# A selective-scan kernel in which TensorE forms part of dt*u*B with diagonal matrices

## The chip, the cores and the metric

The kernel runs on one core of a Trainium2 chip. The metric is the device time of one execution in microseconds (us). A core has five engines that run side by side, each taking its own instructions in order: TensorE (PE, matrix products into PSUM), VectorE (DVE), ScalarE (ACT), GpSimd (POOL) and SyncE (SP, which here only starts transfers). They wait for each other through semaphores.

## What is computed

The reference is one layer of a bidirectional state-space model over 16 sequences of 512 positions with 256 features, followed by a soft mixture of 16 experts. Inside the first half, 512 channels with 16 states each go through a scan along the sequence, once forward and once backward. Cut to what matters:

```python
dA = jnp.einsum('bld,dn->bldn', dt, A)
dB_u = jnp.einsum('bld,bld,bln->bldn', dt, u, B)
...
xs = jnp.cumsum(dB_u * dA_cum, 1) / (dA_cum + 1e-12)
y = jnp.einsum('bldn,bln->bld', xs, C)
```

`dB_u` is, for each state n, the product dt*u of a channel times B of that state, which depends on the position alone. The kernel writes the scan as a recurrence: h = h * exp(dt*A) + dt*u*B at each position, and takes (1 + tanh(...)) * h * C, summed over the states, for the division by `dA_cum + 1e-12`. After it come a gate, an output projection, a layer norm, the experts (dispatch by a softmax over positions, two matrices with a gelu, a third matrix, combination by a softmax over 1024 slots) and a last layer norm.

## The kernel before, in words

A sequence has four *parts*: `scan_part` for forward and backward (r = 0, 1) and for two pairs of channel chunks of 128 (p = 0, 1), in the order (0,0), (1,0), (0,1), (1,1). A part runs over state pairs n = 0, 2, ... 14 and, in each, over its two chunks. One such *step* covers 128 channels x 512 positions x 2 states, and there are 16 x 4 x 16 = 1024 of them. In a step:

- SP loads, once for both chunks, the rows of B and C of two states, spread over 128 partitions: `bs` (three buffers) and `cs` (two buffers), line 352.
- POOL multiplies `db` = du * bs, two states at once, 1024 elements per partition (line 356; three buffers).
- For each of the two states ScalarE makes the decay exp(dt*A) in a PSUM tile `h` (line 361; a ring of three banks) and `th`, a tanh (line 363). VectorE scans in place in h, with db as the term that is added (line 365 forward, 367 backward), and then writes hg = (th + 1) * h (line 370; four buffers of two states).
- POOL multiplies hg by cs in place (line 371).
- TensorE transposes hg by blocks of 128 and adds it up in the PSUM tile `acc` (line 320), two steps after the step that made it (`add_up(2)`). The first step of a chunk also gets u*D by a matmul with a diagonal matrix (line 333).

Everything else is *side work*, written as generators that yield between pieces and are emitted a piece at a time after each step (`beside_scan`): preparation of the next part (`prep_*`: projections, convolution, silu, softplus, and `prep_pair`, which makes dt, rr and, on POOL, du = dt*u), the end of the sequence before with the experts' dispatch (`finish`, `dispatch`), and the experts and the combination (`experts`, `combine`) of pairs of sequences. The side work shares three PSUM banks (`bank`, tag `mps`). A piece says how many banks it takes; `Side.piece` starts it only if, counted from the oldest bank that is still held, no more than three are in use. A piece that ends with HOLD keeps its bank until the generator is taken up again. `late` pins an instruction to program order on its engine; the others may be moved by the framework's scheduler. With the pools `m_acc` (two banks) and `m_h` (three) the eight banks are given out.

`prep_pair` of a part runs during the part before. `project_unit` (line 240) makes `xd`, which holds the rows of B and C, and writes them to DRAM as `bc`, from where `bs` and `cs` are read. `experts` loads its weights into three buffers with the tag `W` (line 644). `combine` gathers the experts' outputs of one sequence from DRAM into one tile `ceo` of 8 x 257 columns (line 814), whose last column is set to one, so that the matmul at line 844 gives the sum of the softmax weights in column 257; VectorE takes its reciprocal (line 853) before it scales (line 854). After the last scan a tail runs with all eight banks: the experts and the combination of the last two sequences.

## Time and profile before

| | |
|---|---|
| runs of the kernel before, us | 5466.05, 5471.18, 5471.56 (median 5471.18) |
| the profiled execution's own time, us | 5474.83 |
| its span, first to last instruction, us | 5473.0 |
| mean granted TensorE clock | 0.859 |
| first db starts, last db starts, us | 47.5, 5166.5 |
| ScalarE waiting for VectorE's hg (line 361 for line 370), us | 609.8 in 488 waits |
| TensorE waiting for POOL's hg (line 320), us | 312.9 in 145 waits |
| SP waiting for POOL before bs and cs (for lines 371 and 356), us | 2542.8 and 940.9 |
| ceo from its issue to its landing, us | 7.0 |

How to read it: the profile lists groups of instructions by line, engine and tile, with total busy time and mean time of one, and the idle time that its engine had just before such an instruction, with what ended it. Busy shares are averages over the span; tables by stretch tell the stages apart. Durations on POOL are rough, matmuls are pipelined, and idle time of an engine that doesn't set the pace costs nothing.

### The profile page before, as it was taken

How to read it: one execution, taken by the hardware profiler on the slowest of the kernel's cores; microseconds unless marked ns; L12 is line 12 of the kernel's file. 1: busy time of each engine (PE TensorE's matmuls, PEld its weight loads, DVE VectorE, ACT ScalarE, POOL GpSimd, SP SyncE). 2: the span in 40 equal slices, each digit the busy share in tenths (PEclk: the TensorE clock that was granted, in tenths of full speed). 3: DMA queues.
4: the chain of work that ended last, by engine and by line, in shares of the span. 5: the costliest groups of instructions: out<-in, count | busy, mean ns of one | idle time of the engine just before them, and what ended most of it. 6: DMA issues, size and time to landing. Idle time of an engine off the chain costs nothing.

```text
span 5473.0 us, 67758 instructions
## 1 busy us (share of the span) xinstructions
PE 4001.2 (73%) x21317; PEld 3106.7 (57%) x21330; DVE 4522.5 (83%) x6212; ACT 4101.0 (75%) x6665; POOL 5003.5 (91%) x2547
## 2 busy tenths in 40 slices
PE   4556656677787777777777777877777776778887
PEld 2434444565555665566556655555655665567656
DVE  6787878889898888888888898989888888888722
ACT  6667777778778777878777887787778787778641
POOL 6999999999999999999999999999999999989700
PEclk7567777888998998889899888988988898999999
DMA  4333333465546664366544655455544666457435
GB/s 131 112 112 123 122 118 121 157 206 186 166 137 193 198 191 150 131 205 208 177 138 157 204 186 170 136 193 193 192 149 136 200 203 189 139 168 250 135 104 174
DMA packets 493949, 897.77 MB, mean 164 GB/s; under 512 B 44403, under 2 KB 291827, under 8 KB 493589
## 3 DMA queue, kind: packets, MB, share of 16 engines
q1 hardware_dynamic: 454836, 851.48, 48.4%
q10 hardware_dynamic: 38752, 41.95, 2.2%
q8 instruction: 169, 2.77, 0.2%
q14 instruction: 192, 1.56, 0.1%
HBM read 832.47 MB, written 60.82 MB: 163 GB/s over the span
## 4 chain that ended last, share of the span: by engine, by line
DVE 33%; ACT 24%; PE 19%; issue 11%; POOL 10%; DMA 3%; SPq 0%; DVEq 0%; ACTq 0%; POOLq 0%
DVE h L367 9%; DVE h L365 8%; DVE hg L370 8%; ACT h L361 5%; ACT th L363 5%; POOL db L356 4%; POOL hg L371 4%; PE acc L320 3%; PE px L247 2%; PE pg L718 2%; DVE rr L302 2%; PE cl L770 2%; ACT L361 2%; PE peo L703 2%; ACT ht L740 1%
## 5 line engine op out<-in xcount | busy, mean ns | idle before, releaser
L356 POOL TENSOR_TENSOR db<-du,bs 128x1024 f32<-128x1024 f32 x1024 | 2424.6, 2368 | 118.9 <-DVE h L365 50.5
L371 POOL TENSOR_TENSOR hg<-hg,cs 128x1024 f32<-128x1024 f32 x1024 | 2422.2, 2365 | 26.2 <-DVE hg L370 17.6
L370 DVE SCALAR_TENSOR_TENSOR hg<-th,h 128x512 f32<-128x512 f32 x2048 | 1349.1, 678 | 253.4 <-ACT th L363 139.7
L320 PE MATMUL acc<-ident,hg 128*128 128x128 f32 x8192 | 1219.4, 302 | 383.9 <-POOL hg L371 312.9
L320 PEld LDWEIGHTS acc<-ident,hg 128*128 128x128 f32 x8192 | 1074.4, 158 | 622.3 <-POOL hg L371 402.3
L367 DVE TENSOR_TENSOR_SCAN h<-h,db 128x512 f32<-128x512 f32 x1024 | 1226.2, 1219 | 191.5 <-ACT h L361 148.3
L365 DVE TENSOR_TENSOR_SCAN h<-h,db 128x512 f32<-128x512 f32 x1024 | 1221.6, 1219 | 181.9 <-ACT h L361 134.1
L361 ACT ACTIVATE h<-dt,A_f 128x512 f32<-128x512 f32 x1024 | 700.0, 684 | 316.6 <-DVE hg L370 313.8
L361 ACT ACTIVATE h<-dt,A_b 128x512 f32<-128x512 f32 x1024 | 699.8, 683 | 297.6 <-DVE hg L370 296.1
L363 ACT ACTIVATE th<-rr,Ah_b 128x512 f32<-128x512 f32 x1024 | 728.0, 711 | 0.3
L363 ACT ACTIVATE th<-rr,Ah_f 128x512 f32<-128x512 f32 x1024 | 726.9, 710 | 0.2
L703 PE MATMUL peo<-Wd,ht 128*128 128x256 f32 x1024 | 321.0, 469 | 196.2 <-DVE ht L687 136.0
L703 PEld LDWEIGHTS peo<-Wd,ht 128*128 128x128 f32 x1024 | 227.4, 232 | 269.7 <-DVE ht L687 143.0
L718 PE MATMUL pg<-st,Wg 128*128 128x128 f32 x2048 | 280.1, 300 | 77.4 <-ACT xb L222 39.7
L770 PE MATMUL cl<-seT,cx 128*128 128x512 f32 x512 | 275.7, 681 | 74.0 <-DVE rr L302 35.7
L718 PEld LDWEIGHTS pg<-st,Wg 128*128 128x128 f32 x2048 | 270.5, 215 | 87.5 <-ACT xb L222 41.2
L675 PE MATMUL pu<-st,Wu 128*128 128x128 f32 x2048 | 268.7, 287 | 30.4 <-ACT ht L740 11.8
L675 PEld LDWEIGHTS pu<-st,Wu 128*128 128x128 f32 x2048 | 256.5, 202 | 52.5 <-ACT ht L740 13.2
L574 PE MATMUL pl<-x2T,seT 128*128 128x512 f32 x512 | 260.0, 632 | 24.3 <-DVE xf L171 14.6
L606 PE MATMUL pq<-dis,xn 128*128 128x256 f32 x1024 | 254.6, 406 | 15.4 <-ACT dis L596 12.7
L844 PE MATMUL cpo<-ceo,ct 128*128 128x257 f32 x1024 | 244.1, 393 | 25.5 <-ACT ct L799 16.4
L606 PEld LDWEIGHTS pq<-dis,xn 128*128 128x128 f32 x1024 | 206.3, 207 | 49.8 <-ACT dis L596 15.6
(147 smaller groups left out, 5149.9 us busy)
## 6 DMA issues: line engine op xcount, KB each, us to landing
bs<-bc SPq DMA_DIRECT2D x512, 512.0 KB, 4.6
cs<-bc SPq DMA_DIRECT2D x512, 512.0 KB, 3.7
Wg<-in_Wg_dram SPq DMA_DIRECT2D x128, 512.0 KB, 5.4
Wu<-in_Wu_dram SPq DMA_DIRECT2D x128, 512.0 KB, 5.8
Wd<-in_Wd_dram SPq DMA_DIRECT2D x128, 512.0 KB, 5.9
bd<-in_bd_dram SPq DMA_DIRECT2D x128, 128.0 KB, 4.7
s_dram<-sl ACTq DMA_DIRECT2D x64, 256.0 KB, 3.0
st<-s_dram SPq DMA_DIRECT2D x128, 128.0 KB, 4.5
```

What stands on the lines that cost most here:

```text
L320: ins = nc.tensor.matmul(accs[c][:, s], hc[:, j, s], ident, is_transpose=True, start=False, stop=(last and j == 1 and lc == NL - 1),)
L356: nc.gpsimd.tensor_tensor(db, du.unsqueeze(1).to_broadcast([P, 2, L]), bs, ALU.mult)
L361: nc.scalar.activation(h, dt, AF.Exp, scale=w["A"][:, c, s])
L363: nc.scalar.activation(th, rr, AF.Tanh, bias=LN_1E12 / 2, scale=w["Ah"][:, c, s])
L365: nc.vector.tensor_tensor_scan(h, h, db[:, j, :], 0.0, ALU.mult, ALU.add)
L367: nc.vector.tensor_tensor_scan(h[:, ::-1], h[:, ::-1], db[:, j, ::-1], 0.0, ALU.mult, ALU.add)
L370: nc.vector.scalar_tensor_tensor(hg[:, j, :], th, 1.0, h, ALU.add, ALU.mult)
L371: nc.gpsimd.tensor_tensor(hg, hg, cs, ALU.mult)
L606: nc.tensor.matmul(pq[:, k * 256 : (k + 1) * 256], xn[:, lc, k * P : (k + 1) * P], dis[:, lc, :], start=(lc == 0), stop=(lc == NL - 1),)
L675: nc.tensor.matmul(pu[:, fc * P : (fc + 1) * P], got["Wu", e][:, k, fc * P : (fc + 1) * P], st[:, k, :, j * SL : (j + 1) * SL], start=(k = ...
L703: nc.tensor.matmul(po[:, :DM], ht[:, fc, :], got["Wd", e][:, fc, :], start=(fc == 0), stop=(fc == NF - 1))
L718: nc.tensor.matmul(pg[:, fc * P : (fc + 1) * P], got["Wg", e][:, k, fc * P : (fc + 1) * P], st[:, k, :, j * SL : (j + 1) * SL], start=(k = ...
```

## The change

In each part two of the sixteen states, 5 and 13 (`DIAG`), no longer get their dt*u*B from POOL. In the state pairs n = 4 and n = 12, `bs` and `db` hold one state (k = 1). The second state's term is made by TensorE: `duT`, the transposed du, times a 128 x 128 matrix with B on its diagonal, for each of four blocks of positions.

- The diagonal matrices stand in DRAM (`diag_dram`). They are cleared once at the start by four transfers from a zero tile on ScalarE's queue. `project_unit` then writes the B rows of the two states onto the diagonals, element by element (1024 elements of 4 bytes), from ScalarE's queue. A pair before its use, SP loads such a set of four blocks as `dg` (128 x 512, one buffer).
- `turn_pair`, a new generator ahead of the other preparation of a part, transposes the part's two du tiles through the banks of the side work; ScalarE copies them to `duT`.
- `by_diagonal` takes a bank of the side work (`hd`) and makes the four matmuls one step ahead of the step that uses them. The planner counts that bank as held (`diags`) until the step is over. In that step ScalarE writes the decay into an SBUF tile `dec` (two buffers) instead of an h tile, and VectorE scans into the bank.
- `combine` takes its experts' outputs in two tiles of four slot groups each, in buffers of the tag `W` (in the tail, in a pool of four). The column of ones is gone: the sum of the weights comes out of the exp itself (`accum_out`), with a small sum and the reciprocal on VectorE in `weights`.
- Tiles of side work (yt, et, sl, the bias rows) share a tag `fr` with two buffers, and the slot embeddings are loaded in two halves into `W` buffers.

```diff
+DIAG = (5, 13)
+DIAG_SIZE = P * (P + 1)
...
+        diag_dram = drams.tile([2, len(DIAG), NL, DIAG_SIZE], F32, name="diag_dram")
...
+        blank = p2.tile([P, 4 * DM], F32, tag="W", name="blank", bufs=3)
+        nc.vector.memset(blank, 0.0)
+        for part in diag_dram.rearrange("r i l (p s) -> (r i) p l s", p=P):
+            nc.scalar.dma_start(part, blank[:, : NL * (P + 1)].rearrange("p (l s) -> p l s", l=NL))
...
+            step = DIAG[1] - DIAG[0]
+            nc.scalar.dma_start(
+                diag_dram[r].rearrange("i l (p s) -> i l p s", p=P)[:, :, :, 0],
+                xd[XB + DIAG[0] : XB + NS : step, :].rearrange("i (l p) -> i l p", p=P),
+            )
...
+        def turn_pair(b, r, p, v):
+
+            yield 2
+            pts = []
+            for c in (2 * p, 2 * p + 1):
+                pt = bank(f"pdu_{b}_{r}_{c}")
+                for lc in range(NL):
+                    s = slice(lc * P, (lc + 1) * P)
+                    nc.tensor.transpose(pt[:, s], v[c][2][:, s], ident)
+                pts.append((c, pt))
+            yield HOLD
+            for c, pt in pts:
+                duT = p4.tile([P, L], F32, tag="duT", name=f"duT_{b}_{r}_{c}", bufs=2)
+                late(nc.scalar.copy(duT, pt))
+                v[c].append(duT)
...
             prep.drain()
-            prep.gens += [[1, g] for g in then]
+            prep.gens += [[1, g] for g in [turn_pair(b, r, p, v)] + then]
...
+            def by_diagonal(n, c):
+
+                diags.append(count[0])
+                made[n, c] = h = bank(f"hd_{b}_{r}_{n}_{c}")
+                for lc in range(NL):
+                    s = slice(lc * P, (lc + 1) * P)
+                    ins = nc.tensor.matmul(h[:, s], v[c][3][:, s], dg[:, s], start=True, stop=True)
+                    if lc == 0:
+                        late(ins)
...
+                k = 1 if n + 1 in DIAG else 2
...
+                if n + 3 in DIAG:
+                    dg = p4.tile([P, L], F32, tag="dg", name=f"dg_{q}", bufs=1)
+                    nc.sync.dma_start(
...
-                    nc.gpsimd.tensor_tensor(db, du.unsqueeze(1).to_broadcast([P, 2, L]), bs, ALU.mult)
+                    nc.gpsimd.tensor_tensor(
+                        db[:, :k, :], du.unsqueeze(1).to_broadcast([P, k, L]), bs[:, :k, :], ALU.mult
+                    )
...
-                        h = ps_h.tile([P, L], F32, tag="h", name=f"h_{q}_{c}_{j}")
-                        nc.scalar.activation(h, dt, AF.Exp, scale=w["A"][:, c, s])
+                        if j < k:
+                            dec = h = ps_h.tile([P, L], F32, tag="h", name=f"h_{q}_{c}_{j}")
+                            add = db[:, j, :]
+                        else:
+                            add = h = made.pop((n + j, c))
+                            dec = p4.tile([P, L], F32, tag="dec", name=f"dec_{q}_{c}", bufs=2)
+                        nc.scalar.activation(dec, dt, AF.Exp, scale=w["A"][:, c, s])
...
+                    nxt_n = n if c == chunks[0] else n + 2
+                    if nxt_n + 1 in DIAG:
+                        for x in sides:
+                            x.take_up()
+                        by_diagonal(nxt_n + 1, chunks[1] if c == chunks[0] else chunks[0])
                     beside_scan()
+                    if k == 1:
+                        diags.pop(0)
...
-                    oldest = min([x.hold for x in sides if x.hold is not None], default=count[0])
+                    oldest = min([x.hold for x in sides if x.hold is not None] + diags[:1], default=count[0])
...
-            for cm, cl in zip(cms, cls):
-                nc.scalar.activation(cm, cl, AF.Exp, bias=nm[:, 2:3])
+            sm = p3.tile([P, 3], F32, tag="csm", name=f"csm_{i}", bufs=2 * NL)
+            for h, (cm, cl) in enumerate(zip(cms, cls)):
+                nc.scalar.activation(cm, cl, AF.Exp, bias=nm[:, 2:3], accum_out=sm[:, h : h + 1])
...
+            for c0 in range(0, NSC, 4):
+                if wide:
+                    t = wide[0].tile([P, 4, DM], F32, tag="ceo", name=f"ceo_{b}_{c0}", bufs=4)
+                else:
+                    t = p2.tile([P, 4 * DM], F32, tag="W", name=f"ceo_{b}_{c0}", bufs=3)
+                    t = t.rearrange("p (c o) -> p c o", c=4)
+                for j in range(2):
+                    nc.sync.dma_start(t[j * SL : (j + 1) * SL, :, :], own[j][:, c0 : c0 + 4, :])
```

## The prediction

> **What bounds the kernel now.** I read the page's list of costliest groups first, then busy time by stretch, then who waited for whom.
>
> ```profile
> PE 4001.2 (73%) x21317; PEld 3106.7 (57%) x21330; DVE 4522.5 (83%) x6212; ACT 4101.0 (75%) x6665; POOL 5003.5 (91%) x2547
> L356 POOL TENSOR_TENSOR db<-du,bs 128x1024 f32<-128x1024 f32 x1024 | 2424.6, 2368 | 118.9 <-DVE h L365 50.5 <-issue 47.8 <-DVE h L367 10.8
> L371 POOL TENSOR_TENSOR hg<-hg,cs 128x1024 f32<-128x1024 f32 x1024 | 2422.2, 2365 | 26.2 <-DVE hg L370 17.6 <-PE cl L770 3.2 <-DVE c_mv L50 2.9
> ```
>
> There are 1024 steps (16 sequences, 64 parts, 16 steps each), and in each POOL spends 2368 + 2365 = 4733 ns on two products. The first db starts at 47.5 us (the db tile's view) and the last hg ends near 5186, so a step takes 5138/1024 = 5.02 us, 94% of it these two; with `du` and small operations POOL is busy about 4982 of 5138 us. Some 156 us are left idle. POOL is the bound, but not in every stretch (columns: stretch, length, busy PE, PEld, DVE, ACT, POOL, clock, DMA share, GB/s):
>
> ```profile
> 3360.00:3440.00 80.00, 66.77 (x317) 46.81 (x318) 75.20 (x106) 62.30 (x103) 80.00 (x38) 0.91 0.38 129
> 3440.00:3520.00 80.00, 57.98 (x279) 40.62 (x279) 69.00 (x93) 64.11 (x103) 77.35 (x42) 0.91 0.47 146
> 3520.00:3600.00 80.00, 59.31 (x313) 43.70 (x312) 69.44 (x99) 65.07 (x109) 73.36 (x38) 0.89 0.40 136
> 3600.00:3680.00 80.00, 59.10 (x385) 51.85 (x384) 67.81 (x95) 63.34 (x101) 79.50 (x46) 0.89 0.60 192
> ```
>
> Two things to see. VectorE can run at 94% (75.20 of 80) with POOL never idle, and its usual share is 85 to 88%. And one stretch in four starves POOL (73.36 of 80): of the 63 such stretches from 80 to 5120 us, 16 have POOL below 94.5%, and in 39 it is at 97% or more. What starves it (timeline: start, length, engine, what), and two lines of the list of waits (total, times, longest):
>
> ```profile
> 3584.20 1.28 ACT L228 ACT_TABLE_LOAD   x1
> 3585.49 1.91 ACT L228 ACTIVATE xb<-xb 128x2048 f32<-128x2048 f32 x1
> 3587.42 1.28 ACT L361 ACT_TABLE_LOAD   x1
> 3589.44 1.23 DVE L365 TENSOR_TENSOR_SCAN h<-h,db 128x512 f32<-128x512 f32 x1 [3.80 <-ACT h L361]
> 3590.81 2.35 POOL L356 TENSOR_TENSOR db<-du,bs 128x1024 f32<-128x1024 f32 x1 [5.05 <-issue]
> ```
>
> ```profile
> DVE hg L370 <- PE acc L320: 44.9, 62, 2.1
> PE cl L770 <- DVE rr L302: 35.7, 12, 4.2
> ```
>
> Two table loads and a silu keep ScalarE from the scan for 4.5 us; VectorE gets its decay 3.80 us late; POOL's next db waits for a free buffer. The waits say that TensorE seldom delays VectorE, but that a tile of side work that finds no free bank waits some 3.9 us (12 events with the weight load: 46.9 us).
>
> **The Trainium skill.** GPSIMD Engine Reference, section Elementwise: a two-input product is held by one shared read port at about 2.6 cycles of 1.2 GHz per element, 2.17 ns. The trace agrees: (2368 - 1272)/512 = 2.14 ns, between a db (1024 elements) and a `du` (512, L304). So half a db is half the work, less a fixed 176 ns. PSUM — Partial Sum Buffer, section Specifications (TRN2): eight banks; the pools of this kernel (3 + 2 + 3) use all, so the new products must borrow from side work. TensorE: Matmul & The Clock Gate, Part 1: the clock is gated down by idleness. The trace fits: 0.62 with TensorE 53% busy (50 to 400 us), 0.91 above; I book no slowdown for more matmuls, and no gain. DMA: Bandwidth & Descriptors, Specifications: below 512 B a write is read-modify-write; no 4-byte write is in this trace.
>
> **Part by part.**
>
> *Removed from POOL.* In two of eight state pairs (n = 4 and 12) db makes one state. That is 64 parts x 2 pairs x 2 chunks = 256 instructions, each now like `du` (1272 ns): 256 x 1096 ns = 280.6 us. Fourteen memsets of 125 ns go: 1.8. Sum 282 us. hg keeps its size.
>
> *Added to TensorE.* 256 groups of four diagonal matmuls. L333 does the same shape: (77.8 + 71.2) us over 128 groups = 1.16 us each, 298 us. 128 tiles of `du` transposed: L512 0.63 us to L591 0.76 us a tile, about 88 us. Together 386 us, 6.0 per part. Cover: TensorE is idle a quarter of the time (windows above: 57.98 to 66.77 of 80). In the busiest, 66.8 + 6 = 73 of the about 76 us that a part would take, there is none.
>
> *Added to ScalarE.* 128 copies duT at 577 ns (L517): 74 us. 128 accumulator reads at 191 ns (as for L585): 24. 256 exps into SBUF instead of PSUM: at most 711 - 684 = 27 ns each, 7. 32 issues of the scattered write into `diag_dram`, about 0.5 us (the `D_f` load, 512 elements of 4 B, took 0.50 to issue): 16; these stand on ScalarE's own queue and first wait for xd; behind them are the softplus and the scan's exps. Sum 121 us, 1.9 per part, free where ScalarE has its 20% of slack, not in the starved stretches.
>
> *VectorE.* 64 small sums at 150 ns, 10 us; the scans keep one operand in SBUF and one in PSUM: zero, bounded by the 2 to 3% between the forms of one row (1194 to 1232 ns) either way.
>
> *DMA and SP.* 128 loads dg (256 KB) against 128 halved bs (256 KB less): no bytes net; 128 + 32 more issues at about 0.4 us on SP, which waits for POOL most of the time. dg is issued with the bs of the pair before and needed a pair later, 9 us against 4 to 6 of landing: hidden. The scattered write: 1024 elements; `D_f` landed in 2.3 us for 512, so I take 3 and bound it by 2 and 10; it has at least two steps before dg reads it. If not, SP is held, and behind dg stand bs and cs.
>
> *Expert outputs in weight buffers.* Two half tiles per sequence instead of one: the first half can arrive before the last experts end. At the end TensorE waits 9.12 us for ceo; I take 3 us of it as gain. The blanks at the start (1 MB, on ScalarE's queue) cost about as much: 3. Both cancel; bound -5 to +6. The next experts' first loads queue behind these buffers: 8 times, up to 5 us, off the path.
>
> *New waits.* (a) A diagonal group waits at the head of TensorE for a bank; queued behind are the transposes of hg, then VectorE's next hg (four buffers). (b) VectorE's second scan waits for the group; behind it its own hg, then POOL. The trace shows neither. Nearest: 62 waits of VectorE for acc, 0.7 us each, and 3.9 us for a blocked bank. The second state no longer takes one of the three h tiles, so something below nothing is possible: from -0.3 us to 3.9 us per group. I take about 0.1 (0.5 us per part outside the stretches named next).
>
> *The sum.* 282 us leave POOL. Given back: in the 16 starved parts the saving (280.6/64 = 4.4 us) is lost, as ScalarE sets the pace there: 70. Their added ScalarE time, 16 x about 1.7: 27. In the eight stretches like the first window the whole saving would need TensorE at 97% and VectorE at 99%; I let 3 of 4.4 go: 24. The other 40 parts, 0.5 each: 20. Sum 141; gain 282 - 141 = 141 us. The profiled execution took 5474.83 us (span 5473.0): 5334. The median of the runs, 5471.18, lies 3.65 lower: **5330 us**. With the last three items halved or doubled, 5260 to 5410.
>
> **Rivals.**
>
> *POOL stays the bound throughout.* VectorE needs 4.35 us a step (4445 busy from 50 to 5200, and 10), POOL then 4.59 (4700). For it: the stretches with POOL at 100% and VectorE at 94%. Against: the starved ones. 5474.8 - 282 = 5193, less 3.65: 5189.
>
> *Another engine takes over whole.* TensorE's busy time in the scan, 3760 (the stretches from 50 to 5200), plus 386, plus its waits for side work's data (L591, L703, L790, L247, others: about 620), plus its waits for POOL at L320 (383): 5149, no better than 5138. Against: such waits shrink when it arrives later. With a small rest of gain: 5460.
>
> *Slower: the borrowed bank.* One mechanism: TensorE stands at the diagonal group because the bank of three still holds side work, and acc, hg and POOL stop behind it. Price 3.9 us an event. If one group in four is hit: 64 x 3.9 = 250, 5330 + 250 = 5580. It decides from 141/3.9 = 36 events of 256 on. For: TensorE is in order and the third bank is often held. Against: the planner counts the diagonal's bank as held when it starts pieces.
>
> That it doesn't do what it says is out: the halved db is a shape in the program.
>
> **Chances.** Forecast 0.53; POOL bound throughout 0.21; taken over 0.10; slower 0.16. About 0.2% (11 us) is what a measurement tells from no change; of the third case I count 0.06 within it. Faster 0.78, same 0.06, slower 0.16. The range reaches from full saving to no change: 5185 to 5480, leaving out the slower case and a little below.
>
> **What would show it.** db in two forms, 768 of 2368 and 256 near 1272 ns; POOL about 4721 us busy and 94% of the scan; TensorE near 4390, ScalarE near 4215; VectorE at 91% or more in the scan; POOL's idle time before db up from 119 to some 250 us, put down to VectorE. Wrong if db's half costs much more than 1272, if the waits of VectorE for the diagonal group or of TensorE before it come to over 140 us, or if TensorE rather than POOL is over 95% busy.

## The result and the profile after

The changed kernel takes 5650.34 us (median of four runs, 5648.91 to 5656.03) against 5470.78 for the kernel before beside it: a ratio of 1.0334, 95% interval 1.0321 to 1.0347. It is 180 us slower where 141 us less were forecast. The busy times of the page of the kernel after:

```profile
span 5649.0 us, 73811 instructions
PE 4239.9 (75%) x23889; PEld 3370.8 (60%) x23890; DVE 4521.0 (80%) x6275; ACT 4169.3 (74%) x6904; POOL 4733.4 (84%) x2537
```

POOL is 270.1 us less busy (5003.5 to 4733.4), and the span is 176 us longer; so POOL's idle time has grown by 446 us. Adding up the idle column over all of POOL's groups gives the same: 465.8 us before, 912.0 after. No engine is busier than 84%. The costliest groups by line, of the kernel after, with the two forms of db first (busy, mean ns, then the engine's idle time before such an instruction and what ended it):

```profile
L406 POOL TENSOR_TENSOR db<-du,bs 128x1024 f32<-128x1024 f32 x768 | 1809.7, 2362 | 178.1 <-issue 68.4 <-DVE h L424 63.2 <-DVE h L422 27.3
L406 POOL TENSOR_TENSOR db<-du,bs 128x512 f32<-128x512 f32 x256 | 326.7, 1276 | 90.6 <-DVE h L422 37.6 <-DVE h L424 30.2 <-issue 19.1
```

```profile
L428 POOL TENSOR_TENSOR hg<-hg,cs 128x1024 f32<-128x1024 f32 x1024 | 2415.9, 2362 | 237.0 <-DVE hg L427 171.8 <-PE cl L839 23.2 <-issue 11.6
L384 PE MATMUL hd<-dg,duT 128*128 128x128 f32 x2048 | 288.4, 286 | 78.0 <-ACT xb L231 35.8 <-ACT et L654 23.9 <-ACT res L246 6.1
L329 PE MATMUL pdu<-ident,du 128*128 128x128 f32 x512 | 86.6, 311 | 64.2 <-ACT ht L809 47.7 <-ACT et L654 13.7 <-POOL du L318 2.5
L334 ACT COPY duT<-pdu 128x512 f32<-128x512 f32 x128 | 67.6, 578 | 39.2 <-PE pdu L329 39.2
```

The half product costs what was forecast (1276 ns). POOL's idle time before db is 269 us, close to the forecast 250; but before hg, where it was 26.2, it is 237.0, and VectorE's hg ends most of it (171.8). The list of waits of the kernel after says who stands for whom (total, times, longest):

```profile
POOL c_rs L53 <- DVE c_mv L52: 349.1, 16, 185.6
ACT th L420 <- DVE hg L427: 339.4, 283, 7.0
ACT h L418 <- DVE hg L427: 304.5, 264, 4.7
POOL hg L428 <- DVE hg L427: 171.8, 105, 5.5
DVE hg L427 <- PE acc L350: 152.7, 98, 5.4
DVE cx L927 <- PE cpo L918: 127.2, 32, 9.9
ACT sl L685 <- PE pq L675: 81.8, 39, 6.7
```

(Most of the first line is the *tail*, the work after the last scan: 185.6 us is one wait there. From 1250 to 5000 us it is 58.2 us in 5 waits, and 0.2 us in the kernel e5 below.) VectorE's waits for acc have grown from 44.9 to 152.7 us. For the new product itself VectorE waits only 45 us (35.7 on the forward line, 9.3 on the backward).

Where in time? Each row is the distance from the first hg of one sequence to that of the next, in us, for the kernel before and after and for two experiments (e5: the short products and the rearranged buffers, with no turn, diagonals or product; e4: the change in the first three sequences only):

```
sequence              1    2    3  |   4    5    6    7    8    9   10   11   12   13   14   15
before              313  316  317  | 317  320  321  320  321  321  321  320  321  321  321  320
after               296  293  298  | 329  334  345  334  345  334  345  334  345  334  345  334
e5 saving, buffers  300  302  302  | 317  319  316  319  316  319  316  319  316  320  317  318
e4 first three      296  293  298  | 316  321  321  319  320  320  321  320  321  321  321  321
```

The break lies between the third and the fourth sequence, where the experts begin to run beside the scan (from 1006 us in the kernel before; the combination from 1423 us, in the fifth). Without them the change gains 20 us a sequence (946 to 887 us over three); with them it loses 18 (3845 to 4060 us over twelve). The tail, from the end of the last hg to the end, has grown as well, from 287 to 304 us: of the 1024 records of the combination's product cpo 224 stand behind the last scan, before it was 171. About three of its 64 blocks have slid out of the scan.

One stall from the latter kind, in the timeline of the kernel after (start, length, engine, line, what, and the idle time before it with what ended it):

```profile
2972.90 5.91 PE L675 MATMUL pq<-dis,xn 128*128 128x256 f32 x16 [1.32 <-ACT dis L665]
2973.07 1.26 POOL L406 TENSOR_TENSOR db<-du,bs 128x512 f32<-128x512 f32 x1
...
2973.55 1.23 DVE L422 TENSOR_TENSOR_SCAN h<-h,db 128x512 f32<-128x512 f32 x1 [0.78 <-ACT h L418]
...
2978.86 1.02 ACT L685 ACTIVATE sl<-pq,norm_b,norm_g 128x256 f32<-128x256 f32 x2 [4.78 <-PE pq L675]
...
2980.31 1.07 ACT L869 COPY ct<-ctp 128x512 f32<-128x512 f32 x2 [0.44 <-ACT sl L685]
...
2980.95 3.72 PE L918 MATMUL cpo<-ceo,ct 128*128 128x256 f32 x16 [1.26 <-ACT ct L869]
...
2984.51 1.04 PE L329 MATMUL pdu<-ident,du 128*128 128x128 f32 x8
...
2984.71 0.48 DVE L927 SCALAR_TENSOR_TENSOR cx<-cpo,csm,cx 128x256 f32<-128x256 f32 x1 [9.93 <-PE cpo L918]
2985.15 1.07 ACT L334 COPY duT<-pdu 128x512 f32<-128x512 f32 x2 [3.76 <-PE pdu L329]
...
2985.96 0.23 POOL L53 TENSOR_SCALAR c_rs<-c_mv 128x4 f32<-128x4 f32 x1 [11.63 <-DVE c_mv L52]
...
2989.79 2.37 POOL L428 TENSOR_TENSOR hg<-hg,cs 128x1024 f32<-128x1024 f32 x1 [1.87 <-issue]
```

Follow it backwards. POOL ends a short db at 2974.33 and begins its next product at 2989.79: in 15.5 us it does four small operations of 1.7 us together. It stood 11.63 us at c_rs, a small piece of the combination, for VectorE's statistics; VectorE stood 9.93 us at cx for TensorE's cpo; TensorE waited for ScalarE's ct; ScalarE had stood 4.78 us at sl for TensorE's pq, a group of 5.9 us. Then it stood 3.76 us more at duT, for a transpose that TensorE had queued behind cpo. From 2974.8 to 2985.3 none of the four runs an instruction of the scan: its instructions stand behind these pieces on all four queues at once. It isn't the whole story: from 1250 to 5000 us POOL waits 59 us at c_rs in e7 below, and nothing in e6, e9 and e17, so it explains none of the loss that these three show.

Last a view that the prediction doesn't use: the chain of work that ended last, by engine, of the kernel before and of the kernel after.

```profile
DVE 33%; ACT 24%; PE 19%; issue 11%; POOL 10%; DMA 3%; SPq 0%; DVEq 0%; ACTq 0%; POOLq 0%
```

```profile
DVE 33%; PE 24%; ACT 24%; issue 12%; POOL 5%; DMA 1%; ACTq 0%; DVEq 0%; SPq 0%; POOLq 0%
```

POOL was 91% busy before, but held 10% of that chain. VectorE, ScalarE and TensorE held 76%. The share is a rough measure: in e4, where POOL is as busy as before from the fourth sequence on, it is 6%.

The granted clock of TensorE doesn't explain the loss: it is 0.870 in the profiled execution of the kernel after, 0.859 in that of the kernel before.

### The profile page after: what moved, and what is told of

Read it like the earlier page. It is cut to its first block, busy times and chain, and to the rows that moved or that the text cites. A ratio compares the mean times of both kernels' runs of the same rounds, so it can differ in the third digit from the quotient of the medians.

```text
span 5649.0 us, 73811 instructions
## 1 busy us (share of the span) xinstructions
PE 4239.9 (75%) x23889; PEld 3370.8 (60%) x23890; DVE 4521.0 (80%) x6275; ACT 4169.3 (74%) x6904; POOL 4733.4 (84%) x2537
## 4 chain that ended last, share of the span: by engine, by line
DVE 33%; PE 24%; ACT 24%; issue 12%; POOL 5%; DMA 1%; ACTq 0%; DVEq 0%; SPq 0%; POOLq 0%
DVE hg L427 8%; DVE h L422 7%; DVE h L424 7%; ACT th L420 4%; ACT h L418 4%; PE acc L350 3%; PE pq L675 3%; PE cpo L918 3%; PE px L256 3%; POOL hg L428 3%; DVE rr L316 2%; PE peo L772 2%; ACT L418 2%; ACT ht L809 2%; DVE hd L422 1%
## 5 line engine op out<-in xcount | busy, mean ns | idle before, releaser
L428 POOL TENSOR_TENSOR hg<-hg,cs 128x1024 f32<-128x1024 f32 x1024 | 2415.9, 2362 | 237.0 <-DVE hg L427 171.8
L406 POOL TENSOR_TENSOR db<-du,bs 128x1024 f32<-128x1024 f32 (+1 forms) x1024 | 2136.4, 2091 | 268.7 <-DVE h L424 93.5
L427 DVE SCALAR_TENSOR_TENSOR hg<-th,h 128x512 f32<-128x512 f32 x1792 | 1184.7, 679 | 285.9 <-PE acc L350 152.7
L350 PE MATMUL acc<-ident,hg 128*128 128x128 f32 x8192 | 1178.6, 294 | 206.5 <-POOL hg L428 170.3
L350 PEld LDWEIGHTS acc<-ident,hg 128*128 128x128 f32 x8192 | 1044.1, 153 | 364.5 <-POOL hg L428 207.9
L424 DVE TENSOR_TENSOR_SCAN h<-h,db 128x512 f32<-128x512 f32 x896 | 1072.9, 1218 | 210.9 <-ACT h L418 193.3
L422 DVE TENSOR_TENSOR_SCAN h<-h,db 128x512 f32<-128x512 f32 x896 | 1067.5, 1218 | 70.6 <-ACT h L418 63.1
L418 ACT ACTIVATE h<-dt,A_f 128x512 f32<-128x512 f32 x896 | 609.2, 680 | 168.4 <-DVE hg L427 164.2
L418 ACT ACTIVATE h<-dt,A_b 128x512 f32<-128x512 f32 x896 | 611.3, 682 | 141.4 <-DVE hg L427 140.3
L384 PE MATMUL hd<-dg,duT 128*128 128x128 f32 x2048 | 288.4, 286 | 78.0 <-ACT xb L231 35.8
L384 PEld LDWEIGHTS hd<-dg,duT 128*128 128x128 f32 x2048 | 261.2, 200 | 89.3 <-ACT xb L231 39.8
L839 PE MATMUL cl<-seT,cx 128*128 128x512 f32 x512 | 267.1, 669 | 19.0 <-DVE rr L316 17.5
L660 PE MATMUL pd<-ident,et 128*128 128x128 f32 x512 | 106.5, 345 | 214.1 <-ACT et L656 188.4
```

The costliest lines, as they stand in the source:

```text
L350: ins = nc.tensor.matmul(accs[c][:, s], hc[:, j, s], ident, is_transpose=True, start=False, stop=(last and j == 1 and lc == NL - 1),)
L384: ins = nc.tensor.matmul(h[:, s], v[c][3][:, s], dg[:, s], start=True, stop=True)
L406: nc.gpsimd.tensor_tensor(db[:, :k, :], du.unsqueeze(1).to_broadcast([P, k, L]), bs[:, :k, :], ALU.mult)
L418: nc.scalar.activation(dec, dt, AF.Exp, scale=w["A"][:, c, s])
L422: nc.vector.tensor_tensor_scan(h, dec, add, 0.0, ALU.mult, ALU.add)
L424: nc.vector.tensor_tensor_scan(h[:, ::-1], dec[:, ::-1], add[:, ::-1], 0.0, ALU.mult, ALU.add)
```

## The experiments

Eighteen kernels ran, each beside the kernel before on the same chip; intervals are 95%, and reach some 6 to 9 us to either side. The kernel before itself took 5466 to 5473 us from chip to chip, so that steps of 13 or 14 us between experiments of different chips are barely told from nothing.

### Parts of the change

**e1**: all of the change but its diagonals, that is the experts' outputs in weight buffers, the shared tag `fr` and the sum out of the exp.

```diff
-DIAG = (5, 13)
+DIAG = ()
-            prep.gens += [[1, g] for g in [turn_pair(b, r, p, v)] + then]
+            prep.gens += [[1, g] for g in then]
```

(and without `diag_dram`, its blanks and its writes)

> The changed kernel without any diagonal: DIAG is empty, so no blank transfers, no turned du, no diagonal matmuls, every db full; what stays is the experts' outputs in weight buffers, the sums out of the exp, the shared fr buffers and the split slot embeddings. Theory A (the diagonal work makes in-order TensorE late, and side work pinned on VectorE and ScalarE then stops the scan): this part is harmless, 5455 to 5490 us. Theory B (the borrowed bank): the same, 5455 to 5490. Theory C (weight loads and experts' outputs share buffers and stop SP and TensorE in the sequences with experts, where all the loss lies): 5600 to 5700 us.

Measured: 5456.0 us, ratio 0.9971 (0.9959 to 0.9983). The rearranged buffers don't cost; they gain some 16 us.

**e2**: the kernel before, with the short product alone (and bs of one state for it); the second state's scan takes the first state's product.

```diff
+                k = 1 if n + 1 in DIAG else 2
...
-                    nc.gpsimd.tensor_tensor(db, du.unsqueeze(1).to_broadcast([P, 2, L]), bs, ALU.mult)
+                    nc.gpsimd.tensor_tensor(
+                        db[:, :k, :], du.unsqueeze(1).to_broadcast([P, k, L]), bs[:, :k, :], ALU.mult
+                    )
...
-                            nc.vector.tensor_tensor_scan(h, h, db[:, j, :], 0.0, ALU.mult, ALU.add)
+                            nc.vector.tensor_tensor_scan(h, h, db[:, min(j, k - 1), :], 0.0, ALU.mult, ALU.add)
```

> The kernel before with only the saving: in the state pairs 4 and 12 db makes one state and the second state's scan adds the first state's product again (so two of sixteen states get the wrong B; the output is not the reference's). Nothing is added on TensorE or ScalarE. If the saving is what the prediction took it for, 5200 to 5330 us. If VectorE and ScalarE cannot go faster than POOL did, so that the saving itself was an illusion in the sequences with experts, 5400 to 5470 us.

Measured: 5376.64 us, 0.9824 (0.9808 to 0.984). The saving, with nothing added for it, is worth 96 of the 282 us, which lies between the two ranges expected. This alone takes two thirds of the forecast's income away.

**e3**: the diagonal product in the ring of h, the planner not told of it.

```diff
-                diags.append(count[0])
-                made[n, c] = h = bank(f"hd_{b}_{r}_{n}_{c}")
+                made[n, c] = h = ps_h.tile([P, L], F32, tag="h", name=f"hd_{b}_{r}_{n}_{c}")
```

> The changed kernel with the diagonal product in the ring of three h tiles instead of a bank of the side work, and the planner not told of it. All added TensorE and ScalarE work stays. Theory B (the borrowed bank makes TensorE wait and holds back side work): most of the loss goes, 5300 to 5420 us. Theory A (the amount of TensorE work): the loss stays, 5580 to 5700 us; the h ring held longer may cost some more.

Measured: 5602.64 us, 1.0241 (1.0225 to 1.0256). Without the borrowed bank 48 us of the loss go and 132 stay: the rival of the prediction had the right sign, and a fifth of the size. And of the 48 us, 29 are in the tail (304 to 275 us), where no diagonal product is made: the combination that had slid behind the last scan is back in it. In the scan itself the borrowed bank, with its count in the plan, cost 19 us.

**e4**: the diagonals in the first three sequences only, which have no experts beside them.

```diff
-            prep.gens += [[1, g] for g in [turn_pair(b, r, p, v)] + then]
+            prep.gens += [[1, g] for g in ([turn_pair(b, r, p, v)] if b < 3 else []) + then]
...
+            diag = DIAG if b < 3 else ()
...
-                k = 1 if n + 1 in DIAG else 2
+                k = 1 if n + 1 in diag else 2
```

> The changed kernel with diagonals in the first three sequences alone, where no experts run beside the scan and where the trace shows a gain of 17 to 26 us each. Theories A and B: the kernel before less some 60 us, 5400 to 5430 us. Theory C: the loss of the sequences with experts stays, 5530 to 5620 us.

Measured: 5401.77 us, 0.987 (0.9856 to 0.9885). It beats both kernels, by 1.3% the kernel before. The table above shows it: the gain of the first three is kept, and from the fourth on it runs like the kernel before.

### A ladder from the saving to the changed kernel

**e7** is the changed kernel but for the reading: the diagonal product is made, and the second state of a short group takes the first's product from POOL.

```diff
-                        if j < k:
-                            dec = h = ps_h.tile([P, L], F32, tag="h", name=f"h_{q}_{c}_{j}")
-                            add = db[:, j, :]
-                        else:
-                            add = h = made.pop((n + j, c))
-                            dec = p4.tile([P, L], F32, tag="dec", name=f"dec_{q}_{c}", bufs=2)
+                        dec = h = ps_h.tile([P, L], F32, tag="h", name=f"h_{q}_{c}_{j}")
+                        add = db[:, min(j, k - 1), :]
```

**e6** also leaves out the product and the transfers, and **e5**, the lowest rung, the turn as well, so that the short product and the rearranged buffers remain. Against e7 (e5: all of it; e6: all but its first two lines):

```diff
-            prep.gens += [[1, g] for g in [turn_pair(b, r, p, v)] + then]
+            prep.gens += [[1, g] for g in then]
-            nc.scalar.dma_start(
-                diag_dram[r].rearrange("i l (p s) -> i l p s", p=P)[:, :, :, 0],
...
-                if n + 3 in DIAG:
-                    dg = p4.tile([P, L], F32, tag="dg", name=f"dg_{q}", bufs=1)
...
-                    if nxt_n + 1 in DIAG:
+                    if False:
```

> The changed kernel with the halved db and the rearranged buffers, and nothing added: no turned du, no dg, no diagonal product; the second state of pairs 4 and 12 adds the first state's product again (two of sixteen states get the wrong B). It is the zero of the ladder: if rearrangement (16 us less than before) and saving (96 us less) add up, 5350 to 5375 us on every theory.

> As saving_rearranged, with the turned du added (128 transposes of a tile on TensorE, 128 copies on ScalarE, pinned, two banks of the side work for a while); nobody reads duT. Theory A (amount of TensorE work; 88 of the 386 us are here): a quarter of the loss of some 290 us, 5410 to 5450 us. Theory D (ScalarE's added copies and their place at the head of each part): more than half of it, 5480 to 5560. Theory E (VectorE's scan waits for TensorE's product through the queues): little, 5360 to 5400.

> The changed kernel with all that it adds on TensorE, ScalarE, SP and the DMA queues, the diagonal product in its borrowed bank and the planner's account of it too, but the scan of the second state doesn't read it: it uses an h tile and the first state's product (two of sixteen states get the wrong B). No instruction of VectorE waits for the product, and its bank is free when TensorE has written it. Theory A (the work itself): 5600 to 5680 us, as the changed kernel. Theory E (the wait of the scan for the product): 5370 to 5470 us.

Measured: e5 5384.2 us (0.9843, 0.9829 to 0.9858); e6 5554.28 (1.0156, 1.0139 to 1.0174); e7 5636.08 (1.0306, 1.0291 to 1.0321). So the turn, reckoned at next to nothing, costs 170 us; that VectorE reads TensorE's product, with the decay in SBUF, adds only 14. e5 is 88 us faster than the kernel before, while 96 (e2) and 16 (e1) would give 112 and the 5350 to 5375 us expected. The two don't add up: the twelve sequences with experts take 3812 us in e5 and 3795 in e2, which has no rearranged buffers. POOL's two products in the page of e5:

```profile
L409 POOL TENSOR_TENSOR hg<-hg,cs 128x1024 f32<-128x1024 f32 x1024 | 2422.5, 2366 | 101.7 <-DVE hg L408 61.0
L391 POOL TENSOR_TENSOR db<-du,bs 128x1024 f32<-128x1024 f32 (+1 forms) x1024 | 2146.1, 2096 | 234.1 <-DVE h L403 113.2
```

Before, these idle times were 26.2 and 118.9. POOL gives 191 us of its saving back by standing at its own two products, most of it for VectorE.

**e8**: the diagonal product in bf16.

```diff
-                duT = p4.tile([P, L], F32, tag="duT", name=f"duT_{b}_{r}_{c}", bufs=2)
+                duT = p4.tile([P, L], BF16, tag="duT", name=f"duT_{b}_{r}_{c}", bufs=2)
...
-                    ins = nc.tensor.matmul(h[:, s], v[c][3][:, s], dg[:, s], start=True, stop=True)
+                    ins = nc.tensor.matmul(h[:, s], v[c][3][:, s], dg[:, s].bitcast(BF16)[:, 1::2], start=True, stop=True)
```

> The changed kernel with the diagonal product taken from bf16 values (duT rounded by the copy, the upper halves of dg), so that one product of four blocks should cost TensorE about 0.3 to 0.5 us instead of 1.1; two of sixteen states lose precision. Everything else stays: waits, banks, order as the scheduler gives it. Theory A (TensorE's added time): some two thirds of the loss go, 5440 to 5530 us. Theory E (the chain of waits through the product): the loss stays but for the shorter product itself, 5600 to 5650 us.

Measured: 5659.81 us, 1.0343 (1.0326 to 1.0361). Its group of the diagonal product:

```profile
L384 PE MATMUL hd<-dg,duT 128*128 128x128 bf16 x1024 | 107.1, 228 | 85.5 <-ACT xb L231 39.9 <-ACT et L654 27.2 <-DVE xf L180 7.2
```

TensorE does it in 107.1 instead of 288.4 us, and the kernel is no faster: it lies above both ranges expected. The amount of TensorE's work isn't what costs.

### What of the turn costs 170 us

Four kernels on e5. **e9** keeps only the turn's place in the plan: a generator that yields as the turn does, counts two banks, and issues nothing. **e10** adds to that the transposes alone, **e11** the copies alone (from du itself), **e12** is the whole turn with the copies free for the scheduler.

Against e6, e9 and e10 (e10: the last three lines only):

```diff
-                pt = bank(f"pdu_{b}_{r}_{c}")
-                for lc in range(NL):
-                    s = slice(lc * P, (lc + 1) * P)
-                    nc.tensor.transpose(pt[:, s], v[c][2][:, s], ident)
-                pts.append((c, pt))
+                count[0] += 1
...
-                duT = p4.tile([P, L], F32, tag="duT", name=f"duT_{b}_{r}_{c}", bufs=2)
-                late(nc.scalar.copy(duT, pt))
-                v[c].append(duT)
```

Against e6, e11:

```diff
-                pt = bank(f"pdu_{b}_{r}_{c}")
-                for lc in range(NL):
-                    s = slice(lc * P, (lc + 1) * P)
-                    nc.tensor.transpose(pt[:, s], v[c][2][:, s], ident)
-                pts.append((c, pt))
+                count[0] += 1
+                pts.append((c, v[c][2]))
```

Against e6, e12:

```diff
-                late(nc.scalar.copy(duT, pt))
+                nc.scalar.copy(duT, pt)
```

> The short product and the rearranged buffers, with the turn as a generator that issues nothing: it takes its place in the plan of the preparation and counts two banks as taken, but there is no transpose and no copy. Leaves out: the second state of each short group is computed with the product of the first. Theory P (the turn costs 170 us because it shifts the other side work in the plan): near 5554, as with the turn. Theories T (TensorE's transposes) and S (ScalarE's copies): near 5384, as without it.

> As the plan alone, and the 512 transposes of the turn on TensorE into two banks, which nothing reads; no copies on ScalarE. Leaves out: as the plan alone. Theory P: near 5554. Theory T (transposes stand at the head of TensorE's queue for a bank or for du, with accumulations behind them): near 5554, against 5384 for the plan alone. Theory S: near 5384 to 5400.

> As the plan alone, and the 128 copies of 128x512 on ScalarE, pinned, from du itself instead of a bank; no transposes. Leaves out: as the plan alone. Theory S (74 us of copies in the queue of exponentials and their waits): near 5500 to 5554. Theory T: near 5384 to 5400. Theory P: near 5554, with no difference to the plan alone.

> The whole turn, transposes and copies, with the copies free to be placed by the scheduler and not pinned at their place in the program. Leaves out: the second state of each short group is computed with the product of the first; the turned tiles are not read. If the pinned place of the copies makes the cost: near 5400. Theories P and T: near 5554. Theory S: 5450 to 5554.

Measured: e9 5500.25 us (1.0053, 1.0037 to 1.007); e10 5491.32 (1.0039, 1.0026 to 1.0052); e11 5511.03 (1.0074, 1.0059 to 1.0089); e12 5498.99 (1.0052, 1.0037 to 1.0067). The place in the plan costs 116 us with no instruction in it. On top of it the transposes cost nothing (-9), the copies 11, both together unpinned nothing (-1), and only the full turn with its copies pinned 54. POOL's two products in the page of e9:

```profile
L401 POOL TENSOR_TENSOR hg<-hg,cs 128x1024 f32<-128x1024 f32 x1024 | 2417.5, 2361 | 158.3 <-DVE hg L400 132.3
L383 POOL TENSOR_TENSOR db<-du,bs 128x1024 f32<-128x1024 f32 (+1 forms) x1024 | 2140.3, 2090 | 290.4 <-DVE h L395 128.9
```

Against e5 the idle time here is 113 us longer (448.7 to 335.8), of the 116. The work is equal; only side work stands at other places. The preparation starts later in every part (its matmuls pz by one or two steps), and POOL's wait for VectorE's hg grows from 61.0 to 132.3 us. Which of the moved pieces makes it isn't told apart.

### Is it this place in the plan, or any?

**e13**: e6, with the turn out of the plan, at the start of a part, in two tiles of the ring of h, copies not pinned. **e14**: the whole change so, with the product in the ring of h as in e3. **e16**: e9's empty turn, planned behind the preparation of its pair instead of ahead of it. **e15**: the whole change with the turn there, four turned tiles in bf16, copies not pinned.

The turn off the plan (e13, e14):

```diff
-            prep.gens += [[1, g] for g in [turn_pair(b, r, p, v)] + then]
+            turn_pair(b, r, p, v)
+            prep.gens += [[1, g] for g in then]
...
-                pt = bank(f"pdu_{b}_{r}_{c}")
+                pt = ps_h.tile([P, L], F32, tag="h", name=f"pdu_{b}_{r}_{c}")
```

The turn behind the preparation (e15, e16):

```diff
-            prep.gens += [[1, g] for g in [turn_pair(b, r, p, v)] + then]
+            prep.gens += [[1, g] for g in then]
...
                 v[c] = [dt, rr, du]
+            yield from turn_pair(b, r, p, v)
```

> The whole turn, 512 transposes and 128 copies, at the start of each part in two tiles of the ring of h, with the plan of the side work told nothing of it, copies not pinned. Leaves out: the second state of each short group is computed with the product of the first; the turned tiles are not read. If the turn's place in the plan was the cost: 5384 to 5420. If its instructions are: 5500 to 5554.

> The whole change, computed in full, with the turn and the diagonal product both in the ring of h and the plan of the side work as in the kernel before. If the plan made the loss: 5400 to 5470, no slower than before. If the added work of TensorE and ScalarE makes it: 5550 to 5650.

> The whole change with the turn planned behind the preparation of its pair, a part earlier (four turned tiles, in bf16 so that they fit, which made no difference to the time before), copies not pinned; the product in the borrowed bank as in the changed kernel. If the preparation's delay made the loss of 170: 5650 less 116 to 170, so 5480 to 5535. If any change of the plan costs the same: 5600 to 5650.

> The short product and the rearranged buffers, with a turn that issues nothing, planned behind the preparation of its pair, two banks counted as taken. Leaves out: the second state of each short group is computed with the product of the first. If what cost 116 us is the preparation coming later: near 5384. If any change of the plan does it: near 5500.

Measured: e13 5543.88 us (1.0139, 1.0124 to 1.0155); e14 5639.65 (1.0315, 1.03 to 1.0331); e15 5619.17 (1.0279, 1.0262 to 1.0296); e16 5405.67 (0.9888, 0.9873 to 0.9903). e16 shows that the place matters: the same empty turn, with the same count of two banks, costs 21 us behind the preparation and 116 ahead of it. In the whole change, though, moving it there gives back only 31 us (e15), not the 116 to 170 that were hoped for. And e13 and e14 overthrow the theory that the plan is the whole cause: with the plan untouched the turn costs 160 us all the same (5544 less 5384), and the whole change is 173 us slower than the kernel before. There the cost is of another kind: in e13 the preparation's pz stands at nearly the same steps as in e5, and the first three sequences, without experts, lose too (918 us against 903 in e5 and 894 in e6). Its groups of the turn, by line:

```profile
L318 PE MATMUL pdu<-ident,du 128*128 128x128 f32 x512 | 93.8, 318 | 70.2 <-DVE hg L404 61.4 <-ACT duT L320 4.7 <-DVE sm L630 2.1
L320 ACT COPY duT<-pdu 128x512 f32<-128x512 f32 x128 | 71.0, 587 | 90.4 <-PE pdu L318 90.3
```

TensorE stands 70 us for a tile of the ring of h to come free, and ScalarE 90 us for TensorE; in e6 the same two are 67.4 (most of it for ScalarE) and 16.9. From 1250 to 5000 us POOL waits 38.3 us at c_rs in e13, the stall of the timeline above, and 0.2 in e5.

### What of the rest, and where

**e17**: e6 with the writes of the diagonals and the loads of dg, but no product. **e18**: e4, with the change, its turn and its writes also in the second part of each later sequence.

e17, against e7:

```diff
-                    if nxt_n + 1 in DIAG:
+                    if False:
```

e18, against e4:

```diff
-            diag = DIAG if b < 3 else ()
+            diag = DIAG if b < 3 or (r, p) == (1, 0) else ()
...
```

> The saving with the turn, the 32 writes of diagonals on ScalarE's queue and the 128 loads of dg on SP's, and no diagonal product. Leaves out: the second state of each short group is computed with the product of the first; what is turned and loaded is not read. If the transfers and their issues make the step of 82 us: near 5636. If TensorE's product and its bank make it: near 5554.

> The change in full in the first three sequences, and from the fourth on in the second of the four parts of each sequence only, where the trace of the changed kernel is 3.4 us shorter than that of the kernel before, while the first and the last part are 10 and 11 us longer. If the loss belongs to those two parts: 5402 less 13 times 3.4, so near 5358. If the loss follows the change wherever it is put in a sequence with experts beside: over 5402, to 5460.

Measured: e17 5567.3 us (1.0171, 1.0155 to 1.0186): the transfers cost 13 us (8 by the ratios to the kernel before), so what e7 adds to e17 costs 69 (5636 less 5567). That is more than the product: also its bank, the bank's count in the planner, and a second `take_up` of the side work in the steps that make it. Some side work stands several steps later than in e17 (the first pq of a pair of sequences at step 36 of 128, not 32 or 33), and 26 of the 69 us are in the tail (278 to 304 us). No run takes these apart; e3, without bank and count, gives 48 back. e18 5493.74 us (1.0034, 1.0023 to 1.0045): 92 us slower than e4, though the change is in one part of four. The 3.4 us of its expectation was a miscount: measured by hg, the second part of the changed kernel is as long as before. Mean length of the four parts of a sequence, first hg to first hg, over the sixth to the thirteenth sequence, in us:

```
part        before    e5    after    e4     e18
first        87.3    85.9   93.2    87.3   87.4
second       76.7    74.9   77.0    76.7   76.6
third        78.9    79.1   82.0    78.5   82.4
fourth       78.0    77.6   87.5    78.0   81.3
```

In e18 the changed part keeps its length, and the two unchanged parts after it are 3.9 and 3.3 us longer: a part passes what it doesn't get done on to the next ones. VectorE's busy time agrees: from e4 to e18 it falls in the second part from 66.6 to 63.7 us and rises in the third from 70.1 to 71.6 and in the fourth from 69.3 to 70.2. The loss doesn't belong to two of the parts.

## Why the prediction was wrong, point by point

**The ladder in one table.** Each row adds one thing; then come the idle column summed over all POOL groups of the profile, and the tail, from the end of the last hg to the end.

```
                                            us     step   POOL idle   tail
kernel before                              5472             466       287
saving and rearranged buffers (e5)         5384     -88     646       275
the turn's place in the plan (e9)          5500    +116     758       274
its transposes and pinned copies (e6)      5554     +54     815       279
writes and loads of diagonals (e17)        5567     +13     823       278
product, bank, count; not read (e7)        5636     +69     895       304
the scan reads it (kernel after)           5650     +14     912       304
```

From e5 on each step and the growth of the idle time agree within 5 us: the loss is POOL waiting, not POOL working. That says who waits, not for what. Another order of the rungs would give other steps, as e13 and e16 show.

**"POOL is the bound."** This failed first. POOL had 156 us of idle time in the scan, which was read as: what leaves POOL leaves the span, but for the stretches that were named. In the first part of an expert sequence before, 87.3 us long, POOL is busy 81.0 and VectorE 74.9; with nothing added (e5) POOL falls by 4.2 to 76.8, VectorE is at 76.3, and the part is 85.9 long, 1.4 us less. The next constraint begins there. It isn't one busy engine, as in the rivals (nothing is full in 85.9 us). What is left is waiting: the round trip through db, scan, hg, POOL, transposes and side work, in queues that are in order. This is read from the waits; no run tests it by itself. The windows from 1300 to 5100 us, 3800 us each, of the kernels before, e5 and after (busy PE, PEld, DVE, ACT, POOL):

```profile
1300.00:5100.00 3800.00, 2892.62 (x15914) 2264.95 (x15926) 3323.19 (x4582) 3025.14 (x4930) 3681.41 (x1854) 0.89 0.55 177
```

```profile
1300.00:5100.00 3800.00, 2937.05 (x16111) 2303.43 (x16121) 3357.32 (x4676) 3055.29 (x5077) 3510.51 (x1856) 0.89 0.54 171
```

```profile
1300.00:5100.00 3800.00, 2927.28 (x16667) 2321.66 (x16668) 3143.54 (x4369) 2911.22 (x4822) 3293.25 (x1743) 0.88 0.52 164
```

POOL 97%, then 92%, then 87%; VectorE 87, 88, 83. So the pace is set by no full engine in the later two, and the signs that were forecast, POOL at 94% of the scan and VectorE at 91% or more, didn't come. The chain of waits pointed that way before: 10% of it on POOL. A stretch with VectorE at 94% and POOL at 100% showed that both can run so together once, not that they can go on.

**"Given back: in the 16 starved parts."** This is the term of the sum that was mis-sized. 70 us for 16 parts and 24 for the heavy stretches were booked, 94 in all; the other 20 and 27 were for the new waits and ScalarE's additions. With nothing added, the saving loses 194 of its 282 us (e5), 186 in e2. In the first three sequences, e5 keeps 42 of 52.5 us (3 x 17.5, the saving per sequence); in the next twelve 33 of 210. (The range beside the sum, 5260 to 5410, isn't what halving or doubling its last three items gives, 5295 to 5401; 5260 needs all four halved.) "Starved" isn't a fourth of the parts: it is nearly all of them, once experts run beside the scan.

**TensorE's added work, covered by its idle quarter.** Its size was right (288.4 + 86.6 = 375 us in the groups against 386; the page's total rose by 239 only, but ends of matmuls are modelled), and its amount didn't matter (e8). What came with it did: the diagonal product, read by nobody, costs 69 us with its bank and its count in the plan, of which 26 are the combination that slid into the tail. Idle time of TensorE is no cover for that. How much is the place of the matmuls in TensorE's queue isn't shown.

**ScalarE's copies, 74 us, free where it has slack.** 67.6 us measured. Once the plan is changed, transposes and copies cost nothing unpinned (e12 against e9), 54 us pinned (e6).

**The turn as a step that is moved.** The prediction costed what the turn issues and booked nothing for its place at the head of the preparation, ahead of all other pieces. That is 116 us here and 21 behind them (e16). It is the largest term that the sum hadn't got: a cost put at nothing, without a reason.

**The new waits.** (b) VectorE for the product: 45 us in the waits, 14 us in the time; (a) TensorE before it: 78 us idle. Together 123 us, below the 140 that were to be the sign of failure. The direct waits were about as small as hoped; the sign looked at the wrong place.

**DMA, expert outputs, VectorE.** Transfers 13 us, small as forecast. The rearranged buffers gain 16 us by themselves (e1), outside the bound of -5 to +6; 13 of them are in the tail (287 to 274 us). The scans' time per instruction is as before (1214 to 1219 ns, before 1219). The short db is 1276 ns, (2362 - 1276)/512 = 2.12 ns per element; that agrees with the 2.17 ns estimated from what the Trainium skill, GPSIMD Engine Reference, section Elementwise, says of two-input products, 2.6 cycles per element.

**"Slower: the borrowed bank."** The right sign, and 5580 nearer than 5330, but by luck: its mechanism accounts for 48 us (e3), 19 of them in the scan, and taking both turn and product out of the borrowed banks (e14) gives 5640.

**What stays open.** Which of the moved pieces makes e9's 116 us; and whether some arrangement gains in the expert sequences. Five arrangements of the whole change ran (the kernel after, e3, e8, e14 and e15): all lie from 5603 to 5660 us. The stall of the timeline accounts for part: c_rs alone makes POOL wait 58 us from 1250 to 5000 us; e3 has no such wait and still loses 132 us. The experts were not moved to another time, so that the blame lies on their presence is inferred from the sequences and e4.

## What to carry to other kernels

An engine that is 97% busy is only worth relieving as far as the next constraint, and here, with in-order queues, that was not the next busiest engine but, as far as the waits tell, their circle. Try the bare saving first (here 96 of 282 us), and read the chain that ended last, where POOL held 10%. In a stretch where several engines are near 90%, an added piece of work isn't priced by its length alone but by what it moves: an empty place in the plan of the side work cost 116 us, and 181 us of TensorE time less gave nothing. Put such a change where there is room: in the three sequences with nothing beside them it gained 20 us each, and the kernel that has it only there (5402 us) was faster than both.

## What the runs showed of the hardware

The 1024 matmuls of the diagonal product leave 2048 records and 288.4 us in float32, 1024 records and 107.1 us in bf16. A write of 1024 scattered elements of 4 bytes takes ScalarE 635 ns to issue (median of 32), where 0.5 us had been estimated from a load of 512. Clearing the diagonals at the start (four transfers of 258 KB) held ScalarE's first work back to 7.4 us from 0.7, once; the first db then starts at 50.0 us, before at 47.5.
